# Four-layer graph network: node-major products, transposes and the projection as quarter-array products, and the last pair in two batches

## The chip, the cores and the metric

The kernel runs on one core of one Trainium2 chip. The metric is the device time of one execution in microseconds; the kernel before takes 2188.04 us (median of three runs, 2187.34 to 2188.36).

## The reference

The input `x` holds 32 batches of 512 nodes with 64 features, `adj` is a sparse 512 x 512 graph with a full diagonal. Each of four layers does `x = x + f(relu(layernorm(x)))`:

```
layer 0   v = h with node 0 set; three times: effects = adj @ v
          h = relu([v, effects] @ W1.T + b1);  v = h @ W2.T + b2
layer 1   twice: z = relu((adj @ z) @ weights[i])
layer 2   8 heads of: h = x @ Wh;  s = (h @ h.T) * adj, zeros to -1e16
          softmax(s) @ h + bh; heads side by side, leaky_relu, and then
          the same attention with W_out (64 columns), leaky_relu
layer 3   h = x @ weight; e = leaky_relu(e_src[i] + e_dst[j]) * adj' (diagonal 1)
          softmax(e) @ h + bias
```

Everything is float32. The attentions dominate: for each batch, 8 heads plus two more, each over a 512 x 512 score matrix.

## The kernel before

Batches go in 16 pairs; the two batches' 64 features lie side by side in the 128 partitions (or in 128 columns). A pair passes these stages, each cut into named jobs:

- `front`, jobs F0 to F32: layers 0 and 1. `ln_relu` is spread over VectorE and GpSimd. `transposed` (L447) turns node-major values into feature-major ones with four full-array transposes; `by_nodes` (L463) multiplies a feature-major tile with a block-diagonal 128 x 128 weight in four full-array products of 128 columns and so returns node-major values; `aggregated` (L452) multiplies with the graph.
- `features_of` (zT, zE) and `Keys` (k0 to k3, Y0 to Y3; products L938, evictions on ScalarE L949).
- Attention units. A `Unit` holds one 128-partition tile with eight slices of 512 scores. A score slice comes from `gram` (L568, and L571 that adds the mask in bfloat16); `maxima` (r, VectorE L577) multiplies with the graph and finds the row maximum, `negate` (m), `exponentials` (x, ScalarE L597), `normalise` (n, VectorE L607 and GpSimd L609), `turn` (t, VectorE L615, transposes in 32 x 32 blocks). Units a to d and g to j are heads, two at a time; f is the output attention; e is layer 3.
- `Two.weigh` (v, L624) multiplies the weights with the values `vq` in tiles of 32 x 64 of the array, eight at once. `Spread.quarter` (jobs ZQ, hQ, lQ) has brought the values into the order of the turned weights by DMA on SP. Then us (L659), w (L665), y (L677), o (`project`, L685) and c (`joined`, L697 and L699).
- `features` (f) sends the joined heads `cat` by DMA to `HH`; `nodes` and `values` (h, H; L714 and L719) make the node-major `hn` from it with TensorE and ScalarE.
- `Ends` takes the output attention of one pair and layer 3 of the pair before together (vAE to vDE, L890), eu, et (`rows`, full-array transposes L441) and er (`residual`).
- `Chain` (oA to oF): layer norm, transposes, the product with layer 3's weights (L747, 132 columns, with both score vectors), `src`, and `dst`, which goes through a TensorE transpose (L776), VectorE (L782) and DRAM to `pd`, read by the scores of unit e on ScalarE (L844).
- For the last pair, unit f is summed alone (O), then layer 3 of pair 14 (L), then layer 3 of pair 15 (L).

The order on every engine is written out by hand: HEAD, then ROUND for each middle pair (`name:lag`, the lag telling which pair the job belongs to), then TAIL. Each engine runs its own instructions in that order. PSUM has two pools of four banks: `s` for scores, `mm` for everything else; `weigh` takes all four `mm` banks, `by_nodes` and `transposed` one, `Keys` and `apply_w` two. All transfers inside the loop are issued on SP. At the start, the biases are loaded by DMAs on ScalarE's queue, and L330 (TensorE) and L331 (VectorE) turn them into columns.

Of the kernel before, what the change touches and what calls it, by code (L numbers as in the profile page):

```python
# [8 lines left out]
F32 = mybir.dt.float32  # L9
# [12 lines left out]
def gnn_stack_kernel(  # L22
# [34 lines left out]
        0.F0 0.biases 0.F1 0.weights 0.joined 0.F2 0.F3 0.F4 0.bjoined 0.F5 0.graph2 0.F6 0.graph1 0.graph3 0.graph0  # L57
        1.F0 0.F7 1.F1 0.F8 0.F9 0.F10 0.F11 0.masks 0.loops2 0.F12 0.factor1 0.F13 0.F14 0.F15 0.F16 1.F2 1.F3 1.F4
        0.F17 0.F18 0.loops1 0.F19 1.F5 0.grams 0.F20 0.vectors 0.F21 1.F6 0.F22 0.F23 0.factor2 0.factor3 0.F24
        0.F25 0.F26 0.F27 0.F28 0.F29 0.F30 1.F7 0.F31 1.F8 0.F32 1.F9 0.zT 0.zE 0.ZQ01 2.F0 0.factor0 0.k0 0.k1  # L60
        1.F10 0.Y0 0.s0a 0.Y1 2.F1 0.r0a 0.r1a 0.s1a 0.r3a 0.m0a 0.r2a 0.s3a 0.m1a 0.x0a 0.s2a 0.r7a 0.r6a 0.s1b
        0.x1a 0.ZQ12 0.s0b 0.ZQ10 0.r4a 0.r5a 0.m2a 0.m3a 0.nAa 0.x3a 0.x2a 0.s0c 0.r3b 0.r2b 0.ZQ02 0.r0b 0.r1b
        0.t0a 0.s3b 0.s2b 0.r1c 0.m0b 0.m1b 0.r6b 0.x1b 0.x0b 0.nBa 0.r7b 0.t1a 0.s1c 0.m3b 0.r5b 0.x3b 0.nAb 0.t2a
        0.ZQ11 0.r4b 0.ZQ00 0.m2b 0.t3a 0.r0c 0.t1b 0.x2b 1.F11 0.s2c 0.r2c 0.nBb 0.t0b 0.r3c 0.t2b 1.F12 1.F13
        0.ZQ03 1.F14 0.t3b 0.m1c 0.s3c 0.vA0 0.r6c 0.vB0 0.r7c 0.m3c 0.m0c 0.x1c 0.vC0 0.vD0 0.r4c 0.r5c 0.s0d 0.x3c
        0.s1d 0.m2c 0.x0c 0.x2c 0.nAc 0.us0 0.nBc 0.w10 0.w00 0.y10 0.t0c 0.s2d 0.t1c 0.r1d 0.k2 0.r0d 0.r2d 0.s3d
        0.r3d 0.t2c 0.r4d 0.m0d 1.F15 0.m1d 0.r6d 0.ZQ13 0.x1d 0.r5d 0.y00 0.r7d 0.m2d 0.m3d 0.x0d 0.x2d 0.x3d 1.F16
        0.nAd 0.o0 0.t3c 1.F17 0.t0d 0.nBd 0.t1d 0.c0 0.t2d 1.F18 0.Y2 0.t3d 0.s1g 0.s0g 0.r3g 1.F19 0.r0g 0.r1g
        1.F20 0.vA1 0.vB1 1.F21 0.r2g 0.vC1 0.m0g 0.vD1 0.s3g 0.m1g 0.us1 0.r6g 0.s2g 0.w11 0.r7g 0.s1h 0.x0g 0.x1g
        0.r5g 0.r4g 0.s0h 0.m2g 0.k3 0.y11 0.m3g 0.w01 0.s2h 2.F2 0.x2g 0.nAg 0.r3h 0.y01 0.r1h 0.r2h 0.r0h 0.x3g  # L70
        0.r4h 0.Y3 0.m1h 0.m0h 0.s3h 0.r5h 0.r6h 0.x1h 0.x0h 0.nBg 1.F22 0.t1g 0.o1 0.m2h 1.F23 0.t2g 0.x2h 0.nAh
        1.F24 0.r7h 0.m3h 0.t0g 0.t0h 0.t3g 1.F25 0.x3h 0.s1i 0.c1 0.nBh 1.F26 0.r3i 0.h0 0.t1h 0.t2h 1.F27 0.s0i
        0.r2i 0.H0 1.F28 0.t3h 0.s2i 1.F29 0.f0 0.m1i 0.vA2 1.F30 0.r0i 1.F31 0.vB2 0.vC2 0.vD2 0.s3i 0.r5i 0.r1i
        0.x1i 0.r4i 0.m0i 0.x0i 0.us2 1.F32 0.hQ0 0.nAi 1.zT 0.r7i 0.m2i 1.ZQ01 2.F3 0.s2j 1.zE 2.F4 0.r6i 0.s0j
        0.r5j 0.w12 1.ZQ02 0.s1j 0.r4j 0.r0j 0.r1j 0.m3i 0.t0i 1.k0 1.k1 0.r3j 0.m2j 1.ZQ12 0.s3j 0.r2j 0.x2i 0.y12
        0.m1j 0.x3i 1.Y0 1.s0a 0.nBi 0.r6j 0.w02 0.m0j 1.s1a 1.Y1 0.r7j 0.x1j 1.r0a 1.s3a 0.y02 0.loops3 1.r1a 0.x0j
        2.F5 0.t1i 0.t2i 2.F6 0.nAj 0.m3j 2.F7 1.r2a 1.r3a 0.x2j 1.m1a 1.ZQ10 1.r6a 0.o2 0.t0j 0.x3j 2.F8 1.ZQ00
        2.F9 1.s2a 0.t3i 1.r7a 1.m0a 0.nBj 0.t1j 0.t2j 2.F10 0.c2 0.t3j 1.s1b 1.x1a 0.vA3 0.vB3 1.ZQ03 1.m3a 3.F0
        1.x0a 1.s0b 1.r3b 1.nAa 1.r4a 1.r2b 1.r5a 1.m1b 1.s2b 1.r1b 1.r0b 1.m0b 1.t0a 1.x3a 0.vC3 1.x1b 0.vD3 3.F1
        1.s0c 1.r4b 1.m2a 1.t1a 1.r5b 1.x0b 0.us3 1.s3b 0.hQ1 1.nAb 1.r1c 0.w13 1.x2a 1.r0c 1.s2c 1.m2b 1.r6b 0.w03  # L80
        1.r7b 1.r4c 1.t1b 1.x2b 1.m3b 1.s1c 0.y13 1.x3b 1.r5c 1.nBa 1.r2c 1.m0c 0.y03 1.x0c 1.r3c 1.nBb 1.t2a 1.t0b
        1.t2b 1.m1c 2.F11 0.o3 0.c3 1.m2c 1.t3b 2.F12 2.F13 0.h1 2.F14 1.s0d 1.t3a 1.s3c 1.x1c 1.r7c 1.r1d 1.r6c
        1.m3c 1.x2c 0.H1 1.r0d 1.vA0 1.vB0 1.vC0 1.m0d 1.vD0 1.x3c 1.s1d 1.nAc 1.nBc 0.f1 1.x0d 1.us0 1.s3d 1.t1c
        1.w00 1.t2c 1.k2 1.s2d 1.r3d 1.r2d 1.y00 0.s0f 1.r7d 1.w10 1.r6d 3.F2 1.ZQ11 1.r4d 0.s1f 1.m1d 1.m3d 1.r5d
        1.t0c 1.x1d 1.m2d 2.F15 1.nAd 1.y10 1.t3c 1.x2d 1.t0d 1.o0 1.x3d 1.t1d 1.nBd 0.r3f 2.F16 1.Y2 0.r2f 0.m1f
        1.t2d 2.F17 0.s2f 1.c0 1.t3d 2.F18 0.r4f 2.F19 2.F20 1.vA1 1.vB1 1.vC1 0.r1f 1.vD1 0.s3f 0.x1f 0.r0f 1.us1
        0.r5f 0.m0f 0.m2f 1.s1g 1.w11 0.x0f 0.x2f 0.r7f 0.r6f 1.r2g 0.m3f 1.s0g 1.ZQ13 1.s3g 1.r3g 0.nAf 2.F21 1.r0g
        1.w01 1.r1g 0.x3f 1.s2g 2.F22 0.nBf 0.loops0 1.m1g 1.r6g 1.m0g 1.y01 1.y11 0.t1f 0.t0f 1.r5g 1.s1h 2.F23
        0.hQ2 1.r4g 1.x0g 1.s0h 2.F24 1.r7g 0.t3f 1.x1g 1.r3h 1.r1h 1.m3g 1.o1 1.m2g 2.F25 1.r0h 1.m0h 1.nAg 1.r2h
        1.m1h 0.t2f 1.x3g 1.x2g 1.s2h 1.c1 1.r5h 1.x0h 0.hQ3 1.nBg 0.vAE 0.vBE 0.vCE 1.r4h 0.vDE 1.s3h 1.m2h 1.x1h  # L90
        0.eu 1.t1g 1.t0g 1.nAh 1.t3g 1.k3 1.r7h 1.Y3 0.et 1.s1i 1.r6h 1.x2h 1.m3h 1.s0i 1.t2g 1.x3h 1.t0h 2.F26
        2.F27 1.r3i 1.s2i 1.r2i 1.nBh 1.r1i 1.r0i 1.m1i 2.F28 1.t1h 0.er 1.h0 1.s3i 1.t2h 1.t3h 1.vA2 1.m0i 1.vB2
# [12 lines left out]
        vD0:0 m2c:0 x2c:0 s1d:0 us0:0 s0d:0 F2:-2 nBc:0 r2d:0 w10:0 r0d:0 w00:0 r3d:0 y10:0 y00:0 s2d:0 m1d:0 x1d:0
# [288 lines left out]
    def ln_relu(xt):  # L394
# [716 lines left out]
```

## Time and profile before

| | |
|---|---|
| profiled execution | 2187.51 us, its span 2185.4 us |
| busy: TensorE, VectorE, ScalarE, GpSimd | 2096.9, 1823.4, 1456.2, 1270.6 us |
| products by nodes (L463), all weights | 111.8 us, 768 rows |
| transposes L447, L441, L714 | 28.2, 18.7, 13.2 us |
| projection L685 | 125.1 us, 1024 rows |
| scores L568 and L571; weighted sums L624 and L890 | 627.2 and 239.0 us; 609.9 us |

The span runs from the first to the last instruction. A row of the profile is one pass over the array: a float32 product has two rows (its two passes), a transpose one. A product's row includes the time in which its results leave the array, so rows of neighbours overlap and their sums hold some time twice. In the rows, `64*64` is the part of the array that a product uses: four such products run at once, eight of `32*64`, one of `128*128`.

### The profile page before, as it was taken

The page shows a single profiled execution, that of the slowest core. Times are in us where ns is not written, and L with a number is a line of the kernel's source. Part 1 is how long each engine was busy: PE and PEld are TensorE (multiplying, and loading weights), DVE is VectorE, ACT ScalarE, POOL GpSimd, SP SyncE. Part 2 cuts the span into 40 slices and gives each one's busy share as a digit, 9 for nine tenths or more (in the row PEclk, how much of TensorE's full clock was granted, in tenths as well). Part 3 has the DMA queues.
Part 4 walks back from the last instruction along what each step waited for, and adds up shares of the span by engine and source line. Part 5 has one row for each costly group of instructions (what it writes and reads, how often), then busy time and mean ns, then how long its engine had stood idle before and what let it go on. Part 6 is the DMA issues. An engine that isn't in the chain of part 4 may idle for free.

```text
span 2185.4 us, 78756 instructions
## 1 busy us (share of the span) xinstructions
PE 2096.9 (96%) x32958; PEld 1165.3 (53%) x32958; DVE 1823.4 (83%) x4113; ACT 1456.2 (67%) x3690; POOL 1270.6 (58%) x2158
## 2 busy tenths in 40 slices
PE   5899999999999999999999999999999999999974
PEld 3455555555555555555555555555555555555433
DVE  3578789889898888989888898988889798899954
ACT  1367557667785766767676686766677676677853
POOL 3355556665765566666556656655666565566533
PEclk9999999999999999999999999999999999999987
DMA  6101111111111111212111121211111121111211
GB/s 130 30 9 26 24 19 37 29 23 35 33 34 27 37 28 22 38 29 38 27 33 27 27 39 29 38 27 30 23 34 33 30 37 29 22 24 31 41 20 31
DMA packets 220711, 69.99 MB, mean 32 GB/s; under 512 B 204484, under 2 KB 213828, under 8 KB 220356
## 3 DMA queue, kind: packets, MB, share of 16 engines
q1 hardware_dynamic: 219600, 64.80, 15.7%
q8 instruction: 258, 4.23, 0.8%
q14 instruction: 97, 0.79, 0.1%
q10 hardware_dynamic: 756, 0.17, 0.0%
HBM read 14.43 MB, written 4.26 MB: 9 GB/s over the span
## 4 chain that ended last, share of the span: by engine, by line
PE 71%; DVE 21%; POOL 3%; ACT 3%; issue 1%; DMA 1%; SPq 0%; ACTq 0%; DVEq 0%; POOLq 0%
PE mm L624 17%; PE s L568 17%; PE mm L452 10%; DVE sm L577 9%; DVE sm L615 8%; PE mm L890 5%; PE s L571 4%; PE mm L685 4%; PE mm L665 4%; PE mm L463 3%; PE mm L938 3%; POOL sm L609 2%; PE mm L498 2%; ACT sm L597 1%; PE mm L447 1%
## 5 line engine op out<-in xcount | busy, mean ns | idle before, releaser
L597 ACT ACTIVATE sm<-sm,nmx 128x512 f32<-128x512 f32 x1280 | 909.5, 717 | 249.8 <-POOL nmx L590 158.8
L609 POOL TENSOR_SCALAR sm<-sm,rs 128x512 f32<-128x512 f32 x1280 | 870.3, 700 | 205.7 <-DVE rs L607 175.1
L577 DVE CUSTOM_DVE_ANT_0 sm<-s,A 128x512 f32<-128x512 f32 x1280 | 818.1, 679 | 140.9 <-PE s L571 134.1
L615 DVE STREAM_TRANSPOSE sm<-sm 128x1024 f32<-128x1024 f32 x640 | 767.9, 1223 | 38.7 <-POOL sm L609 32.9
L568 PE MATMUL s<-ZZ,Y 64*64 64x512 f32 x4096 | 552.3, 601 | 2.8 <-DVE mx L577 2.5
L624 PE MATMUL mm<-sm,vq 32*64 32x256 f32 (+1 forms) x17152 | 499.9, 375 | 34.2 <-DVE sm L615 23.8
L624 PEld LDWEIGHTS mm<-sm,vq 32*64 32x64 f32 x17152 | 393.2, 133 | 157.3 <-issue 72.2
L590 POOL TENSOR_SCALAR nmx<-mx 128x2 f32<-128x2 f32 x640 | 143.5, 231 | 444.6 <-DVE mx L577 399.2
L597 ACT ACTIVATION_READ_ACCUMULATOR sm<-sm,nmx 128x1 f32 x1280 | 247.9, 194 | 0.0
L568 PEld LDWEIGHTS s<-ZZ,Y 64*64 64x64 f32 x4096 | 142.1, 132 | 193.4 <-issue 100.1
L571 PE MATMUL s<-NEGM,I2b 64*64 64x512 bf16 x2304 | 239.0, 377 | 0.0
L659 ACT COPY us<-mm 128x256 f32<-128x256 f32 x256 | 76.7, 385 | 156.6 <-PE mm L624 155.0
L677 ACT ACTIVATE y<-mm,cols 128x512 f32<-128x512 f32 x256 | 159.1, 682 | 29.8 <-PE mm L665 29.6
L452 PE MATMUL mm<-AT,v 128*128 128x512 f32 x384 | 173.9, 596 | 0.0
L571 PEld LDWEIGHTS <-I2b 64*64 64x64 bf16 x2304 | 76.3, 107 | 159.0 <-issue 158.3
L411 POOL TENSOR_TENSOR r<-ve,mhalf 128x8 f32<-128x8 f32 x64 | 106.3, 1661 | 81.3 <-DVE ve L409 81.3
L665 PE MATMUL mm<-us,Wh 64*64 64x512 f32 x1024 | 130.3, 590 | 0.8 <-ACT us L659 0.8
L685 PE MATMUL mm<-y,Wo_sb 128*64 128x256 f32 x1024 | 125.1, 386 | 0.6 <-ACT y L677 0.6
L402 POOL TENSOR_TENSOR xc<-x,nmu 128x512 f32<-128x512 f32 x48 | 50.0, 1042 | 124.6 <-DVE nmu L400 117.9
L452 PEld LDWEIGHTS mm<-AT,v 128*128 128x128 f32 x384 | 71.7, 190 | 94.6 <-issue 83.7
L452 PE MATMUL mm<-AT,z 128*128 128x512 f32 x256 | 120.2, 613 | 1.9 <-DVE z L414 1.2
L890 PE MATMUL mm<-sm,vq 32*64 32x256 f32 x3712 | 110.0, 375 | 4.5 <-DVE sm L615 4.5
(127 smaller groups left out, 1775.6 us busy)
## 6 DMA issues: line engine op xcount, KB each, us to landing
vq<-z SPq DMA_DIRECT2D x512, 32.0 KB
HH<-cat SPq DMA_DIRECT2D x128, 64.0 KB
vq<-hn SPq DMA_DIRECT2D x256, 32.0 KB
vq<-h3n SPq DMA_DIRECT2D x256, 32.0 KB
A<-in_adj_dram SPq DMA_DIRECT2D x5, 1024.0 KB
xt<-in_x_dram SPq DMA_DIRECT2D x32, 128.0 KB
ZZ<-ZZ SPq DMA_DIRECT2D x32, 128.0 KB
out_dram<-xo SPq DMA_DIRECT2D x32, 128.0 KB
```

The costliest lines, as they stand in the source:

```text
L452: nc.tensor.matmul(pe, lhsT=v[:, m].rearrange("p j d -> p (j d)"), rhs=AT[:, m, :], start=(first and m == 0), stop=(m == NT - 1),)
L568: nc.tensor.matmul(pss[half][R[ab], :], lhsT=lhsT, rhs=rhs, start=True, stop=False)
L571: nc.tensor.matmul(pss[half][R[ab], :], lhsT=I2b[R[half], :], rhs=NEGM[R[half], k, :], start=False, stop=True)
L577: nc.vector.tensor_tensor_reduce(self.sm[:, s, :], self.pss.pop(s), self.graph(s), 1.0, -FMAX, ALU.mult, ALU.max, self.small("mx", slice(s ...
L597: nc.scalar.activation(self.sm[:, s, :], self.sm[:, s, :], AF.Exp, bias=self.small("nmx", slice(s, s + 1)), accum_out=self.small("ssum", s ...
L609: nc.gpsimd.tensor_scalar(self.sm[:, s, :], self.sm[:, s, :], self.small("rs", slice(s, s + 1)), 1.0, ALU.mult, ALU.mult)
L615: nc.vector.transpose(out=two, in_=two)
L624: nc.tensor.matmul(self.u[i][R[c], 0 : weights.shape[1] * 32], lhsT=values[32 * i : 32 * i + 32, jb, :], rhs=weights[32 * i : 32 * i + 32, ...
L665: nc.tensor.matmul(self.py[ab][c][r, :], lhsT=Wh2[R[c], self.head(c, ab), r], rhs=self.us[R[c], 2 * ab : 2 * ab + 2].rearrange("p i (s e) ...
L677: nc.scalar.activation(self.y[h], self.py[ab][c], AF.Prelu, bias=cols[:, h : h + 1], alpha=0.01)
L685: nc.tensor.matmul(self.pa[R[half], 0 : N // 2], lhsT=Wo_sb[:, self.head(k, ab), :], rhs=self.y[self.head(k, ab)][:, half * N // 2 : (half ...
L890: nc.tensor.matmul(self.u[i][r, 0 : N // 2], lhsT=values[q, jb, :], rhs=unit.sm[q, :, 32 * jb : 32 * jb + 32], start=(jb == 0), stop=(jb = ...
```

## The change

- `by_nodes`, `transposed`, `Ends.rows` and `Chain.nodes` become products of 64 x 64 quarters of the array with 64 (66) columns: 16 products each (32 in `rows` with both kinds) in place of four (eight). The two batches' results go into two `mm` banks, so every eviction becomes two. Transposes are products with the identity.
- `project` splits each contraction of 128 into two of 64, into two banks; `joined` adds one more bank each time on VectorE.
- For the output attention, `hn` is no longer made by TensorE: VectorE turns `cat` in 32 x 32 blocks (job D), and hQ's transfers read it in pieces of 32 values.
- `dst` is written to DRAM straight from `src`.
- The last pair: output attention and layer 3 work on one batch at a time (`HalfOut`, `HalfLast`), with 128 nodes in the partitions of a score tile, four tiles a unit, their graph rows loaded anew (aO, aL), the values brought through DRAM (`SpreadRows`); their weighted sums use one half of the array's columns.
- The biases are loaded on SP, and HEAD, ROUND and TAIL are written anew.

```diff
     def transposed(z):
-        pt = mm_ps()
+        pts = [mm_ps() for _ in R]
         for t in range(NT):
-            nc.tensor.transpose(pt[:, blk(t)], z[:, t].rearrange("p j d -> p (j d)"), ident)
-        return pt
+            for pt, a in zip(pts, R):
+                for j, r in enumerate(R):
+                    nc.tensor.matmul(pt[r, hblk(t)], lhsT=z[a, t, j, :], rhs=ident[a, a], start=True, stop=True)
+        return pts
+
+    def joined_halves(out_, pts):
+        for a, pt in enumerate(pts):
+            nc.scalar.copy(
+                out_.rearrange("p (t a n) -> p t a n", t=NT, a=2)[:, :, a, :],
+                pt[:, : N // 2].rearrange("p (t n) -> p t n", t=NT),
+            )
...
-    def by_nodes(hT, w):
-        pv = mm_ps()
+    def by_nodes(hT, w, n=D):
+        pvs = [mm_ps() for _ in R]
         for t in range(NT):
-            nc.tensor.matmul(pv[:, blk(t)], lhsT=hT[:, blk(t)], rhs=w, start=True, stop=True)
-        return pv.rearrange("p (t j d) -> p t j d", t=NT, j=2)
+            for ab, out_ in enumerate(R):
+                for pv, r in zip(pvs, R):
+                    nc.tensor.matmul(
+                        pv[out_, t * n : (t + 1) * n], lhsT=hT[r, hblk(2 * t + ab)], rhs=w(r), start=True, stop=True
+                    )
+        return [pv[:, : NT * n].rearrange("p (t d) -> p t d", d=n) for pv in pvs]
...
-                nc.vector.tensor_tensor(
-                    v.rearrange("p t j d -> p t (j d)"),
-                    pv.rearrange("p t j d -> p t (j d)"),
-                    ubc.to_broadcast([P, NT, P]),
-                    ALU.add,
-                )
+            for j, (pv, r) in enumerate(zip(pvs, R)):
...
+                    nc.vector.tensor_tensor(v[:, :, j, :], pv, ubc[:, :, r].to_broadcast([P, NT, D]), ALU.add)
...
         def project(self):
 
-            self.pa = mm_ps()
+            self.pa = [mm_ps() for _ in R]
             order = [(k, ab) for ab in range(2) for k in range(2)]
             for n, (k, ab) in enumerate(order):
                 for half in range(2):
-                    nc.tensor.matmul(
-                        self.pa[R[half], 0 : N // 2],
-                        lhsT=Wo_sb[:, self.head(k, ab), :],
-                        rhs=self.y[self.head(k, ab)][:, half * N // 2 : (half + 1) * N // 2],
...
+                    for pa, r in zip(self.pa, R):
+                        nc.tensor.matmul(
+                            pa[R[half], 0 : N // 2],
+                            lhsT=Wo_sb[r, self.head(k, ab), :],
+                            rhs=self.y[self.head(k, ab)][r, half * N // 2 : (half + 1) * N // 2],
...
         def joined(self):
...
-                nc.vector.tensor_copy(s["cat", self.j], self.pa[:, 0 : N // 2])
-            else:
-                nc.vector.tensor_tensor(s["cat", self.j], self.pa[:, 0 : N // 2], s["cat", self.j], ALU.add)
+                nc.vector.tensor_copy(s["cat", self.j], self.pa.pop()[:, 0 : N // 2])
+            for pa in self.pa:
+                nc.vector.tensor_tensor(s["cat", self.j], pa[:, 0 : N // 2], s["cat", self.j], ALU.add)
...
+        def turned(self):
+            s = state[self.p]
+            s["catT", self.j] = bp.tile([P, N // 2], F32, tag="b", name="catT")
+            nc.vector.transpose(out=s["catT", self.j], in_=s["cat", self.j])
...
         def targets_kept(self):
-            dT = hp.tile([P, 2, P], F32, tag="cat", bufs=1, name="dT")[0 : 2 * NT, 0]
-            nc.vector.tensor_copy(dT, self.pt8[0 : 2 * NT, 0:P])
             dst = dr.tile([2, N], F32, tag="dst", name="dst")
-            nc.sync.dma_start(out=dst.rearrange("j (t q) -> (j t) q", q=P), in_=dT)
+            nc.sync.dma_start(out=dst.rearrange("j (t q) -> q j t", q=P), in_=self.src[:, 2:4, :])
...
+    class SpreadTurned(Spread):
+        def quarter(self, i):
...
+            for k in range(4):
+                half, e = k // 2, k % 2
+                nc.sync.dma_start(
+                    out=self.tile[32 * i : 32 * i + 32, half * JB // 2 : (half + 1) * JB // 2, 32 * e : 32 * e + 32],
+                    in_=self.source(i)[32 * k : 32 * k + 32].rearrange("r (b e) -> r b e", e=32),
+                )
...
+    class Half(Unit):
...
+        def weigh(self, part):
+            if part == 0:
+                self.u = [mm_ps() for _ in range(4)]
+            values = spread[self.p, self.kind, self.j].tile
+            for jb in range(part * JB // 2, (part + 1) * JB // 2):
+                for i in range(4):
+                    q = slice(32 * i, 32 * i + 32)
+                    nc.tensor.matmul(
+                        self.u[i][R[0], 0:P],
+                        lhsT=values[q, jb, :],
+                        rhs=self.sm[q, :, 32 * jb : 32 * jb + 32],
+                        start=(jb == 0),
+                        stop=(jb == JB - 1),
+                    )
```

In ROUND, the jobs around the projection and the targets stand like this (before, then after; the number is the lag):

```
before  o3:1 x2b:0 oC:2 t0b:0 m1c:0 F12:-1 x1c:0 nBb:0 hQ1:1 F13:-1 t1b:0 oT:2 x0c:0 c3:1
after   o3:1 F13:-1 c3:1
before  oF:2 m2d:0 de:2 o0:0 m3d:0 F15:-1 x2d:0 x3d:0 k2:0 F16:-1 nAd:0 ZQ13:0 F17:-1 s2e:2
after   oF:2 s3d:0 x0d:0 r5d:0 r4d:0 r7d:0 m2d:0 r6d:0 m3d:0 w10:0 x2d:0 F15:-1 x3d:0 nAd:0 y10:0
        F16:-1 F17:-1 t3c:0 D1:1 t0d:0 nBd:0 de:2 t1d:0 o0:0 hQ2:1 k2:0 s3e:2
```

In HEAD, the jobs `weights` and F1 now stand ahead of `biases`, where before `biases` stood ahead of F1.

## The prediction

> **What bounds the kernel now.** I read the page first (busy shares, slices, chain), then busy time in one steady round and in the last 85 us, then the timeline of TensorE inside a round, then the first 25 us.
>
> ```profile
> PE 2096.9 (96%) x32958; PEld 1165.3 (53%) x32958; DVE 1823.4 (83%) x4113; ACT 1456.2 (67%) x3690; POOL 1270.6 (58%) x2158
> PE   5899999999999999999999999999999999999974
> DVE  3578789889898888989888898988889798899954
> PE 71%; DVE 21%; POOL 3%; ACT 3%; issue 1%; DMA 1%; SPq 0%; ACTq 0%; DVEq 0%; POOLq 0%
> ```
>
> TensorE is at nine tenths from slice 3 to slice 38 and holds 71% of the chain that ended last; VectorE is second. The first ACT L949 of each pair marks a round: in the timeline it stands at 80.5 us for pair 0, 176.9 for pair 1 and 1977.3 for pair 15, so 14 rounds take 1800.4 us, 128.6 each, and 208.1 us follow the last mark. The two windows below are one round and the end.
>
> ```profile
> 945.60:1074.50 128.90, 128.30 (x2036) 71.53 (x2031) 113.21 (x257) 90.72 (x230) 79.47 (x134) 1.00 0.16 31
> ...
> 2110.00:2120.00 10.00, 3.35 (x11) 0.98 (x10) 2.71 (x9) 2.90 (x5) 0.31 (x2) 0.67 0.36 74
> 2120.00:2130.00 10.00, 7.03 (x38) 2.40 (x38) 7.17 (x25) 8.74 (x23) 3.89 (x11) 0.64 0.15 25
> 2160.00:2170.00 10.00, 0.00 (x0) 0.00 (x0) 6.75 (x20) 8.83 (x22) 3.61 (x9) 0.50 0.29 50
> ```
>
> After the length come PE, PEld, DVE, ACT, POOL. In the round PE is busy 128.30 of 128.90 us, DVE 113.21 (88%). So a microsecond taken from PE's stream is a microsecond of the round until DVE, 15.7 us below, stands in the way. At the end no engine is full: one unit's latencies follow another, and PE's granted clock falls to 0.5.
>
> "Busy" hides what PE loses, since each product's row includes its drain. Start-to-start times show it:
>
> ```profile
> 954.03 1.95 PE L685 MATMUL mm<-y,Wo_sb 128*64 128x256 f32 x16
> 955.91 1.16 PE L463 MATMUL mm<-W1T,hT 128*128 128x128 f32 x8
> 957.00 1.09 PE L938 MATMUL mm<-ZZ,G 64*64 64x256 f32 x16
> 957.91 1.04 PE L568 MATMUL s<-ZZ,Y 64*64 64x512 f32 x8
> 958.77 0.40 PE L571 MATMUL s<-NEGM,I2b 64*64 64x512 bf16 x4
> 958.99 1.04 PE L568 MATMUL s<-ZZ,Y 64*64 64x512 f32 x8
> 959.85 0.40 PE L571 MATMUL s<-NEGM,I2b 64*64 64x512 bf16 x4
> 960.17 1.12 PE L624 MATMUL mm<-sm,vq 32*64 32x256 f32 x32
> ```
>
> Where the tile shape stays, the next group starts when the stream ends: L568 takes 0.86 us for 8 (two waves of four quarters, 0.43 a wave of 512 columns), L571 takes 0.22 to the next L568. Where the shape changes, time is lost: the second L571, before 32\*64, takes 0.32; L463 takes 1.09 for 8 (a pitch of 0.111 is 0.89); L685 takes 1.88 for 16, where eight half-waves of L568 (0.215 each) are 1.72. That is 0.10, 0.20 and 0.16 us. Summing a round by these pitches (352 quarter products of 512 columns at 0.1075, 64 of 256 at 0.054, 144 of L571 at 0.054, 1280 of 32\*64 at 0.027, 46 of 128x512 at 0.43, 64 of L685 at 0.107, 80 small full-array ones at 0.11) gives 119.1 of 128.9 us. The built order has 43 changes of shape in a steady round; they and all true waits share the other 9.8, so 0.23 each at the most.
>
> **The change, part by part (steady round).**
>
> *Products by nodes, transposes, rows.* Trace counts hold two passes per float32 product, one per transpose. Six by_nodes calls lose 8 at 0.111 = 0.89 us and get 32 quarter products of 64 columns, eight waves of four. No row shows such a wave; the nearest is this one, waves of two 128\*64 tiles with 64 columns:
>
> ```profile
> 47.59 1.15 PE L376 MATMUL mm<-WT 128*64 128x64 f32 x32 [0.67 <-ACT WT L372]
> ```
>
> The groups' mean durations (the second number after the bar) of a by_nodes product and of the bias-like mask product:
>
> ```profile
> L463 PE MATMUL mm<-W1T,hT 128*128 128x128 f32 x384 | 56.3, 290 | 2.4 <-ACT hT L502 2.3
> L571 PE MATMUL s<-NEGM,I2b 64*64 64x512 bf16 x2304 | 239.0, 377 | 0.0
> ```
>
> 1.15 less the last one's 0.225 is 0.93 us over 16 waves, 0.058 a wave. Lower bound: an eighth of L568's wave, 0.054. Upper bound: L376's 29 ns per instruction, 0.116 a wave. I take 0.058, since L571's four starts fit into 0.40 - 0.377 = 0.023 us: starts on different quarters do not hold each other up. Then by_nodes costs 0.46, -0.43 each, -2.6 a round. Three transposes go from 4 x 0.109 to 0.46, +0.1; nodes (L747) from 0.90 to 0.48, -0.4; rows (L441) from 0.87 to 16 waves = 0.93, +0.1; L714 and L776 go, -0.5. The projection streams the same columns (16 x 0.107 against 8 waves x 0.215): 0. Sum **-3.3**; by the upper bound of the wave (96 waves x 0.058 more) +2.3.
>
> A rule speaks against this. The Trainium skill, "TensorE: Matmul & The Clock Gate" (Wait — 56ns, not 53.3ns?), says that starts never come closer than about 25 ns however small the product, and "TensorEngine Tiling (Array Packing)" (Instruction Overhead) says not to tile a dimension that is already small. By it 384 instructions cost 9.6 us instead of 5.6, and this part would give +0.7 instead of -3.3; L571's 0.023 us over three gaps (8 ns) disagrees for products on different quarters.
>
> *Changes of shape.* With all small work and the projection in 64\*64, the built order has 24 a round instead of 43. 19 x 0.20 = **-3.8** (0.10 to 0.23 by the rows above: -1.9 to -4.4). I take the L463 row, since most that go are between 128\*128 and 64\*64.
>
> *VectorE.* Four joins a round become eight operations (L697 and L699: 0.39): +1.56. Two turns of cat, 128x256: L615's 1.22 for 1024 columns gives 0.31 as a lower bound, L699's whole 0.39 as the upper: +0.8. Five evictions split in two (L490 0.668 against 2 x 0.39, and the like): +0.5. dT goes (-0.27), xo and x3 are joined in one each (-0.3). Sum +2.3: 113.2 becomes 115.5. It lies beside PE and costs nothing while the round stays above it; at 121.8 us DVE's 15.7 us of idle are 6.3. ScalarE: three copies, v and z split (+0.2 each), hn goes (-0.73): +0.2 of 90.7, hidden.
>
> *Waits added.* Products that took one of the four mm banks now take two, and their release needs two evictions; weigh takes all four. In the order, the median distance between a bank's release and its next user falls from 8.5 jobs to 5, and users within 3 jobs go from 9 to 16. Behind a waiting product stand the scores of the next unit, for which DVE's maxima wait; DVE at 95% then evicts later still. Lower bound 0; upper bound the whole gain, 7.1. Before, the same pool shows next to no idle time before L463 (2.4 us in all), so I take 1.5.
>
> *Queues.* SP's count a round hardly changes: the four quarters of hQ read catT in pieces of 128 bytes, dst is written from src without PE and VectorE (4-byte pieces), still ahead of pd on SP, where hQ transfers stand behind that wait. pd's distance to its first user s3e grows from about 13 jobs to 24, and ACT waited for pd 3 times, 10.6 us in all, before; DMA is busy 0.16. I take 0, with an upper bound of 0.7 a round (10.6 over 15 pairs).
>
> Round: -3.3 - 3.8 + 1.5 = **-5.6**, to 123.0 us. 14 rounds: -78.
>
> *Start.* VectorE's L331 stands ahead of L407 and waits for the biases:
>
> ```profile
> 14.76 0.25 PE L330 MATMUL mm<-ident,early 12*128 12x12 f32 x1 [14.76 <-DMA early<-in_L_gnn_bh_dram]
> 15.52 0.68 DVE L407 TENSOR_REDUCE v<-sq 128x8 f32<-128x512 f32 x1
> ```
>
> sq was ready at 7.9 us. The change puts F1 ahead of the biases and their loads on SP: up to 15.5 - 7.9 = 7.6 us earlier, then shorter steps but two evictions each. Between 0 and -9; I take **-8**. The first round holds 3.4 us more of PE's stream and fewer changes of shape: **+2**.
>
> *Last pair.* From the last join (L699 at 2109.2) to the end are 76 us, one serial chain over a whole pair. By batches, batch 0's output attention runs before that join and batch 1's chain has half of each unit's tiles: twice 4 maxima x 0.61 and 4 normalisations x 0.68 less, half the layer norm (-3), no src transfers (-3.5): -16.8. The sums fill only half of the array (32 waves of 128 columns, 3.4 us at full clock and 6.8 at 0.5, against 5.7 now): about 0. A values' way through DRAM lies beside scores. Bounds -25 (DVE's 36.8 us in the last 85 leave room) and 0 (all work of pair 14's last unit collides). I take **-17**.
>
> Sum: -78 - 8 + 2 - 17 = -101. The profiled execution is 2187.51 us (span 2185.4), 0.5 below the median 2188.04. Forecast **2087 us**.
>
> **Rivals.**
> *VectorE and the banks bound the round*: at 126.5 (DVE at 91%) a round gives -2.1; -29 - 23 = 2135. For it: 88% already, fewer spare banks. Against: 2030 to 2060 us show DVE at 94 to 100%.
> *Small waves cost 0.116*: +5.6 a round cancels the gain; only the ends remain, 2165. For it: the L376 row; against: L571's starts.
> *The last pair gains nothing*, since halves fill half the array and pair 14's unit collides: 2104.
> *Slower*: every two-bank product (6 by_nodes, 3 transposes, nodes, rows, 4 projections: 15 a round) waits for its second eviction behind VectorE's queue. Without the 1.5 a round gains 7.1; with 23 us from the ends, a wait of (7.1 + 1.6) / 15 = 0.58 us per product breaks even, about one L577. At 0.7 us: 14 x 3.4 - 23 = +25, 2212. Against: before, DVE's evictions of by_nodes made PE wait almost nowhere.
>
> **How the numbers follow.** Forecast 0.53, banks and VectorE 0.18, no gain at the end 0.09, costly waves 0.07, slower 0.10, no measurable difference (within 0.2%, 4 us, about what a measurement here can tell) 0.03. The forecast's own range is 2060 to 2112 (shape changes 0.10 to 0.23, waits 0 to 3). Leaving out costly waves, slower and no difference leaves 0.80 inside 2050 to 2150; the low end is waits 0, changes 0.23 and -25 at the end (2187.5 - 108 - 6 - 25 = 2048). Faster 0.87, same 0.03, slower 0.10.
>
> **What would show it.** After: rounds of 122 to 124 us; by_nodes' 32 products starting within 0.46 to 0.5 us; DVE near 115 us a round and over 92%; first L447-like product near 12 us; less than 65 us from the last join to the end. Wrong: waves of 0.1 us, PE idle before by_nodes or the projection released by VectorE's evictions, or DVE without idle time in a round above 125.

## The result, and the profile after

| | before | after |
|---|---|---|
| median of the runs | 2187.69 us (2186.71 to 2188.36) | 2245.55 us (2240.55 to 2248.01) |
| profiled span | 2185.4 us | 2242.5 us |

The ratio is 1.0262 (95% interval 1.0243 to 1.0281): the change made the kernel 2.6% slower, where 4.6% faster was forecast. Cut at the first ScalarE copy of the keys of each pair (L1088 now, L949 before), the span goes into four parts:

| part | before | after | forecast | with dst turned by VectorE (below) |
|---|---|---|---|---|
| start, to the mark of pair 0 | 80.5 | 74.4 (-6.1) | -8 | 75.1 (-5.4) |
| first round | 96.4 | 96.4 (0) | +2 | 96.8 (+0.4) |
| 14 rounds | 1800.4 | 1860.3 (+59.9) | -78 | 1751.5 (-48.9) |
| behind the last mark | 208.1 | 211.4 (+3.3) | -17 | 198.3 (-9.8) |

A steady round takes 133.1 us (the median; the mean of the 14 is 132.9), not 123.0 (before: 128.6). The loss is in the rounds, but for 3.3 us behind them. The busy times of the page do not show it: TensorE is busy 43 us less than before. The chain that ended last does.

From the page of after, the busy times, TensorE in the 40 slices, and the first two lines of the chain that ended last:

```profile
PE 2054.0 (92%) x38721; PEld 1218.3 (54%) x38721; DVE 1865.4 (83%) x4239; ACT 1455.9 (65%) x3748; POOL 1275.9 (57%) x2160
...
PE   6899998989989898998989989898998989999885
...
PE 69%; DVE 13%; DMA 8%; issue 3%; ACT 2%; SPq 2%; POOL 2%; DVEq 0%; ACTq 0%; POOLq 0%
PE s L586 18%; PE mm L642 17%; PE mm L468 9%; DVE sm L595 5%; PE mm L863 5%; DMA dst<-src 4%; PE s L589 4%; PE mm L683 4%; PE mm L704 4%; DVE sm L633 4%; PE mm L1077 2%; PE mm L481 2%; PE mm L514 2%; PE mm L456 1%; DMA pd<-dst 1%
```

TensorE's row, nines from slice 3 to 38 before, now has an eight in better than every third place, and transfers, 1% of the chain before, hold 8%, half of it the store of dst (L586, L642 and L595 are the scores, weighted sums and maxima). The waits of after (what waited for what: us in total, times, longest) name who stands behind it:

```profile
ACT s L817 <- DMA pd<-dst: 130.6, 14, 10.7
...
DVE sm L595 <- ACT s L817: 109.5, 19, 8.6
...
PE mm L642 <- ACT Y L1088: 85.3, 13, 8.2
```

SP's own waits name what stands ahead of the load of `pd`:

```profile
SPq L813 <- DMA dst<-src: 114.7, 13, 10.2
```

One round in the timeline of after (start, duration, engine and line, in brackets the idle time before and its releaser):

```profile
1009.48 2.67 SPq L781 DMA_DIRECT2D src<-src  x4
1012.19 0.60 SPq L788 DMA_DIRECT2D dst<-src  x1
...
1021.25 1.13 SPq L813 DMA_DIRECT2D pd<-dst  x2
...
1025.61 1.30 ACT L817 ACTIVATE s<-pd,src 128x512 f32<-128x512 f32 x2 [8.83 <-DMA pd<-dst]
...
1026.33 0.69 DVE L595 CUSTOM_DVE_ANT_0 sm<-s,A 128x512 f32<-128x512 f32 x1 [6.71 <-ACT s L817]
1026.85 1.06 ACT L1088 COPY Y<-mm 128x512 f32<-128x512 f32 x2
...
1027.57 6.32 PE L642 MATMUL mm<-sm,vq 32*64 32x256 f32 x128 [6.37 <-ACT Y L1088]
```

SP issues the store of dst at 1012.19 and can issue the load of pd only at 1021.25, 9.1 us later, since that load waits for the store's end (8.6 to 10.9 us in the 15 pairs). Before, with dst in rows of 512 bytes, the two stood 1.4 us apart:

```profile
1002.85 0.45 SPq L784 DMA_DIRECT2D dst<-dT  x1
1004.28 1.13 SPq L840 DMA_DIRECT2D pd<-dst  x2
```

In after, ScalarE then waits 8.83 us at its first score of unit e; behind that score on ScalarE stands the copy of the keys Y, and TensorE stands 6.37 us for it. The same stretch by windows of 5 us (length, then busy time of PE, PEld, DVE, ACT, POOL, the clock granted to TensorE, the share of the DMA engines, GB/s), then six microseconds of it, and then the whole round:

```profile
1015.00:1020.00 5.00, 4.22 (x87) 2.61 (x89) 4.38 (x7) 1.43 (x3) 2.81 (x5) 1.00 0.00 0
1020.00:1025.00 5.00, 1.20 (x16) 0.22 (x8) 0.00 (x0) 0.00 (x0) 0.00 (x0) 1.00 0.39 62
1025.00:1030.00 5.00, 2.44 (x42) 1.71 (x50) 3.63 (x11) 4.39 (x8) 0.21 (x1) 0.57 0.49 94
1030.00:1035.00 5.00, 5.00 (x106) 2.56 (x90) 4.08 (x14) 5.00 (x13) 2.47 (x5) 0.75 0.29 49
...
1026.00:1032.00 6.00, 4.43 (x82) 2.92 (x90) 5.63 (x17) 6.00 (x13) 0.43 (x2) 0.50 0.46 87
...
959.20:1092.40 133.20, 125.63 (x2402) 73.93 (x2398) 115.33 (x264) 90.58 (x233) 79.23 (x134) 0.97 0.17 30
```

From 1020 to 1025 us VectorE, ScalarE and GpSimd do nothing at all, and in the next two windows TensorE is granted 0.57 and 0.75 of its clock; from 1026 to 1032 us it is one half. The trace shows a half clock at this place in 13 of the 14 rounds, for 6.8 us in eleven of them; the first of the 14, ahead of the first store, has none and took 123.0 us. What the store does in the meantime is not in the row of the DMA engines: their share is 0.00 from 1015 to 1020 us. The packets themselves are quick (1049 of 4 bytes start between 1013 and 1014 us, nearly all of 7 to 9 ns); SP is held until 1021.25, 7 us longer.

### The profile page after: what moved, and what is told of

It reads as the page before. It is cut to its first block, busy times and chain, and to the rows that moved or that the text cites. A ratio compares the mean times of both kernels' runs of the same rounds, so it can differ in the third digit from the quotient of the medians.

```text
span 2242.5 us, 90408 instructions
## 1 busy us (share of the span) xinstructions
PE 2054.0 (92%) x38721; PEld 1218.3 (54%) x38721; DVE 1865.4 (83%) x4239; ACT 1455.9 (65%) x3748; POOL 1275.9 (57%) x2160
## 4 chain that ended last, share of the span: by engine, by line
PE 69%; DVE 13%; DMA 8%; issue 3%; ACT 2%; SPq 2%; POOL 2%; DVEq 0%; ACTq 0%; POOLq 0%
PE s L586 18%; PE mm L642 17%; PE mm L468 9%; DVE sm L595 5%; PE mm L863 5%; DMA dst<-src 4%; PE s L589 4%; PE mm L683 4%; PE mm L704 4%; DVE sm L633 4%; PE mm L1077 2%; PE mm L481 2%; PE mm L514 2%; PE mm L456 1%; DMA pd<-dst 1%
## 5 line engine op out<-in xcount | busy, mean ns | idle before, releaser
L595 DVE CUSTOM_DVE_ANT_0 sm<-s,A 128x512 f32<-128x512 f32 x1264 | 806.7, 678 | 174.5 <-ACT s L817 109.5
L642 PE MATMUL mm<-sm,vq 32*64 32x256 f32 (+1 forms) x16640 | 509.4, 390 | 88.1 <-ACT Y L1088 85.3
L586 PE MATMUL s<-ZZ,Y 64*64 64x512 f32 x4096 | 568.9, 599 | 5.0 <-DVE mx L595 4.1
L642 PEld LDWEIGHTS mm<-sm,vq 32*64 32x64 f32 x16640 | 412.9, 138 | 199.3 <-issue 159.7
L589 PE MATMUL s<-NEGM,I2b 64*64 64x512 bf16 x2288 | 260.8, 377 | 0.1
L586 PEld LDWEIGHTS s<-ZZ,Y 64*64 64x64 f32 x4096 | 154.6, 133 | 174.2 <-issue 80.6
L589 PEld LDWEIGHTS <-I2b 64*64 64x64 bf16 x2288 | 87.0, 107 | 148.8 <-issue 146.8
L817 ACT ACTIVATE s<-pd,src 128x512 f32<-128x512 f32 x120 | 77.1, 680 | 138.9 <-DMA pd<-dst 130.6
L704 PE MATMUL mm<-y,Wo_sb 64*64 64x256 f32 x2048 | 126.7, 380 | 0.0
L415 POOL TENSOR_TENSOR r<-ve,mhalf 128x8 f32<-128x8 f32 (+1 forms) x65 | 107.5, 1653 | 33.0 <-DVE ve L413 26.5
L406 POOL TENSOR_TENSOR xc<-x,nmu 128x512 f32<-128x512 f32 (+1 forms) x49 | 55.6, 1134 | 110.2 <-DVE nmu L404 104.9
```

Source lines behind the costliest of these rows:

```text
L586: nc.tensor.matmul(pss[half][R[ab], :], lhsT=lhsT, rhs=rhs, start=True, stop=False)
L589: nc.tensor.matmul(pss[half][R[ab], :], lhsT=I2b[R[half], :], rhs=NEGM[R[half], k, :], start=False, stop=True)
L595: nc.vector.tensor_tensor_reduce(self.sm[:, s, :], self.pss.pop(s), self.graph(s), 1.0, -FMAX, ALU.mult, ALU.max, self.small("mx", slice(s ...
L642: nc.tensor.matmul(self.u[i][R[c], 0 : weights.shape[1] * 32], lhsT=values[32 * i : 32 * i + 32, jb, :], rhs=weights[32 * i : 32 * i + 32, ...
L704: nc.tensor.matmul(pa[R[half], 0 : N // 2], lhsT=Wo_sb[r, self.head(k, ab), :], rhs=self.y[self.head(k, ab)][r, half * N // 2 : (half + 1) ...
```

## The experiments

**The store undone in two ways, and done alone.** First, after with dst back through a TensorE transpose (a job oD, put back into the order), a VectorE copy and rows of 512 bytes:

```
         def targets_kept(self):
+            dT = hp.tile([P, 2, P], F32, tag="cat", bufs=1, name="dT")[0 : 2 * NT, 0]
+            nc.vector.tensor_copy(dT, self.pt8[0 : 2 * NT, 0:P])
-            nc.sync.dma_start(out=dst.rearrange("j (t q) -> q j t", q=P), in_=self.src[:, 2:4, :])
+            nc.sync.dma_start(out=dst.rearrange("j (t q) -> (j t) q", q=P), in_=dT)
```

> The changed kernel with one part undone: the targets go through a TensorE transpose, a VectorE copy and a transfer of 512-byte rows again, three VectorE jobs after the source copy. Theory A (the store of dst in 4-byte pieces is what lengthens the round: SP waits 8.9 us for it, ScalarE's first L817 then waits for pd, and all engines stand still from 1018 to 1025 us of the round shown): the wait for pd goes, TensorE's clock stays at 1.00 in a round, rounds fall from 133.2 to 123.5 to 125 us and the time to 2100 to 2130 us, below both kernels. Theory B (two banks per product and a fuller VectorE bound the round): the store is beside the point, TensorE and VectorE get more work, rounds stay at 131 us or above, time 2215 us or above.

Measured: 2122.64 us (2121.68 to 2128.11), ratio to before 0.9712 (0.9696 to 0.9729); steady rounds of 124.3 us. That is theory A's range, and theory B falls.

Second, src in the first 16 columns of a 128 x 32 tile, turned by VectorE in 32 x 32 blocks, and four transfers of rows of 128 bytes:

```
+            nc.vector.transpose(out=dT, in_=src32)
+            for a in range(4):
+                nc.sync.dma_start(
+                    out=dst.rearrange("j (t a r) -> a (j t) r", a=4, r=32)[a], in_=dT[32 * a + 8 : 32 * a + 16]
+                )
```

> The changed kernel, with the targets turned by VectorE in 32 x 32 blocks (one transpose of 128x32, about 0.15 us) and stored in four transfers of 8 rows of 128 bytes each; TensorE gets nothing. Theory A: as the run with the TensorE transpose, rounds 123 to 124.5 us, 2095 to 2125 us, a few us below it since TensorE loses no change of shape (two of 0.2 us a round) and VectorE no 0.27 us copy. Theory B: rounds 131 us or above, 2215 us or above.

Measured: 2123.08 us (2122.14 to 2126.36), ratio 0.9709 (0.9694 to 0.9723); rounds of 124.3 us: the same as the first, not a few us below it (VectorE's turn takes 0.21 us). In the timeline of this kernel, the same place as above:

```profile
969.60 1.47 SPq L793 DMA_DIRECT2D dst<-dT  x4
972.16 1.14 SPq L820 DMA_DIRECT2D pd<-dst  x2
...
975.83 1.30 ACT L824 ACTIVATE s<-pd,src 128x512 f32<-128x512 f32 x2 [1.69 <-DMA pd<-dst]
```

2.6 us from the store to the load, though the store is now four transfers, and ScalarE waits 1.69 us, not 8.83. Third, the kernel before with nothing but the direct store:

```
-            nc.sync.dma_start(out=dst.rearrange("j (t q) -> (j t) q", q=P), in_=dT)
+            nc.sync.dma_start(out=dst.rearrange("j (t q) -> q j t", q=P), in_=self.src[:, 2:4, :])
```

> The kernel before with this one part of the change alone: dst is stored straight from src in 4-byte pieces, the transpose L776 and the copy L782 go; the order stays. Theory A: the store takes 8.9 us where the one before let SP go on after 2.8 us at the most; the order leaves 13 jobs (about 5 us) before the first user of pd, so ScalarE waits 3 to 7 us in each of 15 rounds and the time is 2230 to 2290 us. Theory B: the store is hidden or nearly so, 2183 to 2195 us.

Measured: 2327.27 us (2325.57 to 2331.27), ratio 1.0642 (1.0626 to 1.0658); 14 rounds of 137.3 us, 8.7 more than before and above what theory A gave it. In its timeline the store and the load of pd are again 9.2 us apart:

```profile
1049.54 0.60 SPq L779 DMA_DIRECT2D dst<-src  x1
1058.75 1.13 SPq L835 DMA_DIRECT2D pd<-dst  x2
```

So the store alone turns the result: it costs 140 us in the old kernel (2327.27 against 2187.30 in the same experiment) and 123 in the new one (2245.55 against 2122.64), and without it the rest of the change saves 2.9%.

**Issued earlier.** After, with the store ahead of the four transfers of src on SP:

```
+            nc.sync.dma_start(out=dst.rearrange("j (t q) -> q j t", q=P), in_=self.src[:, 2:4, :])
             s["src"] = st.tile([P, NS], F32, tag="src", bufs=2, name="src")
             for j in range(2):
...
         def targets_kept(self):
-            nc.sync.dma_start(out=dst.rearrange("j (t q) -> q j t", q=P), in_=self.src[:, 2:4, :])
```

> The kernel after (2245.6 us) with one edit: the 4-byte store of dst is issued ahead of the four transfers of src, not behind them; the order on the other engines stays. In the trace of after these four take SP 2.7 us (4 issues of about 0.65). Theory A (the wait for the store's end is what a round loses): the store ends up to 2.7 us earlier, ScalarE's wait for pd falls from 8.8 to about 6, rounds fall from 133.1 to 130 to 131 us, so 14 x 2.7 = 38 us less: 2195 to 2220 us. Rival B (the pieces clog the queues, so that what stands behind them is late instead: src itself, which the same scores need): no gain, 2238 to 2255 us.

Measured: 2217.90 us (2216.94 to 2219.91), ratio 1.0142 (1.0127 to 1.0157). ScalarE's wait falls from 130.6 to 103.3 us (ACT s L818 <- DMA pd<-dst: 103.3 us in 14 waits), the mean of the 14 rounds from 132.9 to 131.0, so of the 2.7 us that the store starts earlier 1.9 reach the round. Most of the rest is lost in the store: from it to the load of pd it is now 10.4 us on average, where it was 9.7. The wait is on the path.

**The store with nobody waiting.** The kernel of the first experiment and, behind the loads of pd, the 4-byte store once more, into memory that nobody reads (`src0` is the tile that the transfers of src read):

```
             for j, r in enumerate(R):
                 nc.sync.dma_start(out=self.pd[r], in_=s["dst"][j].partition_broadcast(D))
+            nc.sync.dma_start(out=spare.rearrange("j (t q) -> q j t", q=P), in_=s["src0"][:, 2:4, :])
```

> The kernel after with the targets through TensorE and rows of 512 bytes again (2122.6 us), plus one more store of the same targets in 4-byte pieces straight from src, into an array that nobody reads, issued behind the loads of pd. Nothing of the computation is left out. Theory A (only the wait of pd's load, and of ScalarE behind it, for the end of the store costs time): the store stands beside other work, so 2120 to 2132 us, and rounds of 124 to 125 us. Rival B (1024 pieces of 4 bytes fill the transfer queues and slow whatever is sent beside or behind them, here the quarters of lQ and hQ): rounds of 128 us and more, 2180 us or above.

Measured: 2198.56 us (2197.03 to 2201.95), ratio 1.0054 (1.0039 to 1.0069). Theory A, as far as it said that only the wait costs, falls: 76 us are lost where nobody waits for the store, and rival B's numbers are met. Its transfers and its windows:

```profile
999.76 0.59 SPq L824 DMA_DIRECT2D spare<-src  x1
1000.45 2.72 SPq L930 DMA_DIRECT2D vq<-catT  x4
1003.26 1.09 SPq L236 DMA_DIRECT2D xt<-in_x_dram  x2
1004.40 8.29 SPq L930 DMA_DIRECT2D vq<-catT  x4
```

```profile
998.20:1003.20 5.00, 4.22 (x68) 2.24 (x69) 4.76 (x7) 3.20 (x7) 3.73 (x6) 1.00 0.35 67
1003.20:1008.20 5.00, 2.38 (x38) 1.12 (x31) 2.57 (x7) 1.03 (x3) 0.00 (x0) 1.00 0.87 31
1008.20:1013.20 5.00, 4.01 (x71) 3.40 (x79) 2.47 (x9) 3.23 (x6) 0.21 (x1) 0.67 0.74 59
```

The DMA engines are 0.87 busy while they move less than half as much as in the window before. Behind each of the first twelve of these stores, the slowest packet of 128 or 256 bytes took 2.1 to 4.2 us; the slow ones lie within about 11 us of the store's issue, the time that the store of after holds SP. In the kernel without this store their mean is 0.013 and 0.022 us. Four issues that take SP 2.6 us take 8.29. The engines slow down together there, and in part with nothing in the trace that they wait for:

```profile
1007.42 1.07 ACT L1099 COPY Y<-mm 128x512 f32<-128x512 f32 x2 [3.97 <-remote]
...
1010.60 4.63 PE L642 MATMUL mm<-sm,vq 32*64 32x256 f32 x106 [0.99 <-issue]
```

ScalarE's copy of Y needs a product of TensorE, and TensorE's last product ahead of it had started at 1005.15 and took 0.38 us; TensorE's pause of 0.99 us lies in the middle of one group of like products. Whether the loads of instructions stand in the same jam (16 kB each, 1.0 us as a rule, up to 4.4 in this run) was not tried and stays open.

**Where the pieces land.** The same idle store with its 1024 pieces 512, 64 and 16 bytes apart, and as 128 pieces of 32 bytes:

```
-            spare = dr.tile([2, N], F32, tag="spare", name="spare")
+            spare = dr.tile([2, N, P], F32, tag="spare", name="spare")
+            nc.sync.dma_start(out=spare.rearrange("j (t q) e -> q j t e", q=P)[:, :, :, 0], in_=s["src0"][:, 2:4, :])
...
+            spare = dr.tile([P, 2, NT], F32, tag="spare", name="spare")
+            nc.sync.dma_start(out=spare, in_=s["src0"][:, 2:4, :])
```

The first form is that of 512 bytes; for 64 and 16 the last dimension of `spare` is 16 and 4. The second form is that of 128 pieces.

> The kernel with the idle 4-byte store (2198.6 us, rounds of 129 to 133; without that store 2122.6 us), with one edit: the 1024 pieces of the idle store go to places 512 bytes apart, not to 4 kB in a row. Nothing of the computation is left out. Theory P (the number of pieces sets the price, wherever they land): 2185 to 2210 us. Theory L (the price comes from many small writes into the same few lines of memory): 2120 to 2145 us.

> The kernel with the idle store (2198.6 us; without it 2122.6 us), with one edit: the same 4 kB leave src as 128 pieces of 32 bytes, one from each partition, into 4 kB in a row. Theory P (number of pieces): an eighth of 76 us, so 2125 to 2140 us. Theory L (small writes into the same lines): 4 instead of 16 or more writes share each 128 bytes, so about an eighth to a quarter, 2125 to 2145 us. Rival (any such store behind pd's loads holds up the quarters of hQ and lQ, whatever its pieces): 2180 us or more.

> The kernel with the idle store of 1024 pieces of 4 bytes; here they land 64 bytes apart (4 bytes apart: 2198.6 us; 512 bytes apart: 2123.7 us). If pieces only hold each other up within the same 64 bytes, 2118 to 2130 us; if the stretch that they share is 128 bytes or more, the cost is between, by the number that share it (2 of 32 at 128 bytes: about 2125 to 2140; 8 of 128 at 512 bytes: 2135 us or more).

> The same with the pieces 16 bytes apart. If the price goes with the number of pieces that share a stretch of memory, it is a quarter or less of the 76 us: 2125 to 2145 us. If any two that share a stretch cost the full price of their turn, however many they are, 2170 to 2200 us. If only pieces that touch are held up, 2118 to 2126 us.

| idle store | time (range) | ratio to before |
|---|---|---|
| none | 2122.64 (2121.68 to 2128.11) | 0.9712 (0.9696 to 0.9729) |
| 1024 x 4 bytes in a row | 2198.56 (2197.03 to 2201.95) | 1.0054 (1.0039 to 1.0069) |
| 16 bytes apart | 2124.26 (2123.76 to 2127.53) | 0.9717 (0.9701 to 0.9733) |
| 64 bytes apart | 2122.61 (2119.30 to 2128.60) | 0.9709 (0.9689 to 0.9728) |
| 512 bytes apart | 2123.67 (2119.92 to 2128.88) | 0.9711 (0.9693 to 0.9728) |
| 128 x 32 bytes in a row | 2120.26 (2119.07 to 2121.66) | 0.9694 (0.9679 to 0.9708) |

Theory P falls, and theory L stands, though the 128 pieces came out below the ranges of both. The lines of the DMA queue in the pages (packets, MB, share of 16 engines) of the store in a row and of the one 512 bytes apart have the same number of packets and the same bytes:

```profile
q1 hardware_dynamic: 272368, 68.60, 19.8%
```

```profile
q1 hardware_dynamic: 272368, 68.60, 17.7%
```

In the second, the four issues behind the store take SP their usual 2.55 us, and the window that follows has TensorE at 5.00 of 5.00 at full clock:

```profile
974.31 0.59 SPq L824 DMA_DIRECT2D spare<-src  x1
...
979.64 2.55 SPq L932 DMA_DIRECT2D vq<-catT  x4
```

```profile
977.80:982.80 5.00, 5.00 (x134) 3.37 (x134) 4.96 (x16) 3.99 (x8) 0.21 (x1) 1.00 0.46 89
```

So it is not the number of small writes. 1024 of them into 4 kB of DRAM cost; the same number into 16 kB or more does not, nor do 128 writes of 32 bytes into 4 kB in a row. Nor does the price fall in step with the crowding: at 16 bytes apart, a quarter of the pieces still falls into each stretch, and they cost 1.6 us of the 76, less than the spread of the runs. Whether it counts that the pieces touch, or that more than some number of them fall into one stretch of memory, and what they contend for there, is not told apart by these runs.

**The products and the projection undone, one at a time**, in the kernel with dst turned by VectorE. By_nodes as four full-array products into one bank:

```
-            pvs = by_nodes(hT, lambda r: W2T[r, r])
+            pvs = by_nodes_full(hT, W2T)
```

> The kernel with dst turned by VectorE (2123.1 us, rounds of 124.3), and in it the six by_nodes calls of a round as before: four full-array products of 128 columns into one bank; the evictions stay two each. The stream of TensorE grows by 2.56 us a round, and the built order has 34 changes of tile shape instead of 24. By the prediction's steps: +2.6 and 10 x 0.20, so rounds of 128.5 to 129.3 us and 2180 to 2195 us. Rival (the waits for second banks ate the gain of the small products, which is why a round is 124.3 and not 123.0): one bank less per call gives back 1.3 us or more, rounds of 127 us or less, 2165 us or less.

Measured: 2170.48 us (2167.65 to 2173.67), ratio 0.9920 (0.9903 to 0.9936); rounds of 127.2. The small products are worth 47 us, 2.9 a round, between the prediction's 4.6 and the rival's 2.7 or less. And the projection with its contraction of 128:

```
-            self.pa = [mm_ps() for _ in R]
+            self.pa = [mm_ps()]
...
-                            lhsT=Wo_sb[r, self.head(k, ab), :],
-                            rhs=self.y[self.head(k, ab)][r, half * N // 2 : (half + 1) * N // 2],
+                        lhsT=Wo_sb[:, self.head(k, ab), :],
+                        rhs=self.y[self.head(k, ab)][:, half * N // 2 : (half + 1) * N // 2],
```

> The kernel with dst turned by VectorE (2123.1 us, rounds of 124.3), and in it the projection as before: 8 products with a contraction of 128 into one bank, and one operation of VectorE less in each join. The stream is the same; the built order has 30 changes of tile shape instead of 24. By the prediction's steps (0.20 a change, the joins hidden): +1.2 us a round, rounds of about 125.5, 2135 to 2145 us. Rival (two banks and 1.56 us more of VectorE a round cost as much as six changes of shape): 2118 to 2126 us, or faster.

Measured: 2120.98 us (2118.63 to 2122.12), ratio 0.9696 (0.9682 to 0.9711); rounds of 124.1. The rival is right: this part of the change gains nothing.

One round of each (the first has by_nodes undone, the second the projection, the third neither):

```profile
940.50:1067.60 127.10, 126.32 (x2258) 73.30 (x2254) 115.99 (x265) 90.41 (x233) 79.24 (x134) 1.00 0.15 32
```

```profile
1040.90:1165.50 124.60, 123.50 (x2337) 70.28 (x2334) 113.51 (x259) 90.40 (x233) 78.74 (x134) 1.00 0.15 32
```

```profile
916.40:1040.90 124.50, 123.25 (x2404) 73.46 (x2398) 115.25 (x265) 90.50 (x233) 79.54 (x134) 1.00 0.15 33
```

Busy times cannot tell what the changes of tile shape cost. For that I took, at each change in a round, the time from the first product of one shape to the first of the next, less the stream of what stands between (columns at the full-clock pitches, divided by the tiles that run at once). Over a round these times add up to the round less its stream, so every wait is in them:

| kernel, one round | changes | lost at them | each | stream |
|---|---|---|---|---|
| before, 128.9 | 43 | 10.7 | 0.25 | 118.2 |
| by_nodes undone, 127.1 | 34 | 9.6 | 0.28 | 117.5 |
| projection undone, 124.6 | 30 | 8.9 | 0.30 | 115.7 |
| dst turned by VectorE, 124.4 | 24 | 9.1 | 0.38 | 115.3 |

From 43 to 24 changes 1.6 us go, 0.08 each. The streams are estimates, good to some half a microsecond (the prediction's own sum for the kernel before is 119.1, with which 0.7 us would go, 0.04 each). The fewer the changes, the more is lost at each. So what remains there is not a fixed price of a shape; that it is waits is argued, not shown.

**A better version.** Dst turned by VectorE, the projection as before, the transfers of dst issued ahead of those of src, and in TAIL the first scores of unit e behind the keys:

```
-  ... 11.s1e 13.t1d 13.t3d ... 13.k2 ... 13.Y2 ... 12.s0e 14.t0c ... 12.s3e 14.Y2
+  ... 13.k2 13.Y2 11.s1e 13.t1d 13.t3d ... 14.t0c ... 14.Y2 12.s0e 12.s3e
```

> The kernel with dst turned by VectorE and the projection as before (2121.0 us), with two edits of order: the four transfers of dst are issued ahead of those of src, and in the tail the scores of layer 3 of pairs 11 and 12 stand behind the keys Y2 of the same stretch, where before they stood ahead of them and ScalarE waited for pd with Y2 behind it. In the trace with dst turned by VectorE, ScalarE waits for pd 22.5 us in all, and TensorE stands 4.5 us before a product that waits for Y2 in the round of 131.8 us. Theory (these waits lie on the path): that round falls to 127 or so and the sum to 2108 to 2117 us. Rival (VectorE at 92 to 97% bounds those rounds anyway, and the waits only move): 2118 to 2124 us.

Measured: 2114.28 us (2108.04 to 2117.26), ratio 0.9658 (0.9637 to 0.9679), 3.4% under the kernel before. The waits for pd fall to 12.4 us, and the long round from 134.2 us (projection undone alone) to 130.4, not to the 127 of the theory; VectorE is busy 18.31 of 20 us at the place of the former stall. The interval lies just under that of the projection undone alone (0.9682 to 0.9711), so of this step little more than its sign is certain.

## Why the prediction was wrong, point by point

- ***Queues*: wrong, and this step decides.** It said "I take 0, with an upper bound of 0.7 a round". Measured: 8.8 a steady round (133.1 against 124.3), 123 us in all (2245.55 against 2122.64). It counted the issues on SP and the jobs between pd and s3e, and it took the upper bound from waits for rows of 512 bytes, which take 1.4 us from store to load. The transfer whose form the change altered was named ("4-byte pieces") and given no duration. "24 jobs" was no measure of time either: the first score of unit e was ready 4.6 us after the store was issued (1025.61 - 8.83 - 1012.19), less than the store takes. And the bound looked at ScalarE's wait alone: behind s3e stands Y, behind Y TensorE, and behind the idle time the halved clock. No rival held this; the rival on the slower side named waits for second evictions, and those are not what after shows.
- **Products: right.** -3.3 forecast for the stream, -2.9 measured (118.2 to 115.3). In the timeline of after, by_nodes' 32 products start within 0.47 us (0.46 forecast) and the projection's within 1.73 (1.72):

```profile
960.96 0.64 PE L481 MATMUL mm<-W1T,hT 64*64 64x64 f32 x32
961.43 1.04 PE L586 MATMUL s<-ZZ,Y 64*64 64x512 f32 x8
...
968.02 1.94 PE L704 MATMUL mm<-y,Wo_sb 64*64 64x256 f32 x32
969.75 0.68 PE L481 MATMUL mm<-W1T,hT 64*64 64x64 f32 x32
```

  That is 15 ns a product on four quarters in turn, on average, so the floor of 25 ns between starts in the Trainium skill, "TensorE: Matmul & The Clock Gate" (Wait — 56ns, not 53.3ns?), did not hold between products on different quarters here.
- **Changes of shape and waits of the banks: the mechanism half right, the size too large.** 24 changes, as counted. Forecast -3.8 + 1.5 = -2.3 a round, that is 0.12 for each of the 19 changes that go, net of the waits; measured -0.7 to -1.6, or 0.04 to 0.08 each. Whether the 0.20 was too high or the 1.5 too low, the runs do not tell apart: each that undoes a part takes away banks, and brings back changes of shape, at once.
- **VectorE: the size right.** 115.5 us a round forecast, 115.33 in after; without the store 93% of the round (115.25 of 124.50). The one run that bears on its cost is the projection undone: 1.6 us less of VectorE a round, a bank less and six changes more came out even, so that it is wholly hidden is not shown.
- **Round: 124.3 once the store is undone, 123.0 forecast.** Right within 1.3 us. But the forecast gave this to all 14, and the last two stayed at 131.8 and 127.7 (130.1 and 128.3 before), about 13 us short together: TAIL has its own order, and its rounds were not read.
- **Start: nearly right.** -8 forecast, -6.1 in after. The first transposes stand at 12.69 us (20.41 before; "near 12" forecast). First round: +2 forecast, 0.
- **Last pair: right in sign, too large.** -17 forecast, -9.8 without the store. From the last join to the end 76.2 us became 70.3 (2051.4 to 2121.7), not "less than 65": the two batches' layer norms and evictions still follow one another (TensorE waits 13.2 us, in two waits, for the layer norms' result).

Without the store, the forecast of -101 us would have met -64 us (the spans of the traces): the sign right, and 2122.6 us inside 2050 to 2150, but above the 2060 to 2112 that the forecast gave its own steps.

## What to carry to other kernels

When a change alters the form of a transfer that somebody waits for, price that transfer by itself, from issue to the issue that waits for it, before counting the instructions that it saves. Writing a turned tile to DRAM element by element saved a transpose and a copy here (0.27 us of VectorE) and took 9 us, where rows of 512 bytes took 1.4. What cost nothing that these runs can tell: turning it on an engine first (rows of 128 bytes), pieces of 32 bytes from each partition, or single elements that land 16 bytes apart or more. And the time lost at a place, divided by the number of such places, is not the price of taking one away.

## What the runs showed of the hardware

- 1024 writes of 4 bytes into a row of 4 kB of DRAM take 8.6 to 10.9 us from issue to the load that waits for their end, though the packets leave in about 1 us; what is sent behind them crawls (up to 4.2 us for 256 bytes). The Trainium skill, "DMA: Bandwidth & Descriptors" (Why small descriptors are slow (HBM only)), puts the price of small transfers on a fixed overhead of each packet and each descriptor; here the same 1024 descriptors, 16 bytes apart or more, cost nothing that these runs can tell (2122.6 to 2124.3 us against 2122.6).
- The four transfers of src, 1024 pieces of 4 bytes from SBUF to SBUF, are in every kernel here and showed no such jam: with dst turned by VectorE, the transfers of dst and pd stand right behind them, 2.6 us from the one to the other.
- In the round shown, TensorE was granted half its clock from 1026 to 1032 us, behind 6.4 us of idle time. So a wait cost more than its length: 8.8 us a round against some 6.4 us of idle time. Over the whole execution the granted clock was 0.962 in after and 0.986 without the store.
